# Layer-norm tails that stay in the pixel layout, with bias rows as matmul operands

## Chip, cores and metric

One core of one Trainium2 chip. The metric is the device time of one execution, in microseconds. Engines: PE (matmuls and transposes, with PEld for its weight loads), DVE (vector), ACT (activations), POOL and SP (which issues most DMAs).

## What is computed

Two layers on an input x of 2 x 256 x 128 x 128, both with a residual. The change touches the first layer:

```python
def _branch(x, w_off, w_def, lw, lb, pad, dil):
    off = _conv(x, w_off, pad, dil)
    y = _deform_dw(x, off, w_def, pad, dil)
    return jax.nn.gelu(_ln2d(y, lw, lb), approximate=False)
x1 = _branch(x, off_w1, def_w1, bw1, bb1, 1, 1)
x2 = _branch(x, off_w2, def_w2, bw2, bb2, 9, 9)
x3 = _branch(x, off_w3, def_w3, bw3, bb3, 12, 12)
c = jnp.einsum('bchw,oc->bohw', x, conv_w[:, :, 0, 0]) + conv_b[None, :, None, None]
out = _ln2d(x1 + x2 + x3 + c, n1_w, n1_b)
h = out.transpose(0, 2, 3, 1)
h = jax.nn.gelu(h @ mlp_w1.T + mlp_b1, approximate=False) @ mlp_w2.T + mlp_b2
out = _ln2d(h.transpose(0, 3, 1, 2) + out, n2_w, n2_b)
```

`_ln2d` normalises each pixel over its 256 channels. `_deform_dw` samples nine taps per pixel at learned offsets. The inputs hold bw1 to bw3, n1_w and n2_w at one and bb1 to bb3, n1_b and n2_b at zero. The second layer is a 3x3 convolution with ternary weights.

## The kernel before

The program has three stages. **Phase A** (L286 to 445, image after image) normalises x, writes a padded table of pixels to HBM, computes the offsets and stores "hats", the bilinear weights. A short serial part (`missing`) finds pixels whose offsets lie outside the fast path's reach and computes a flag that chooses between a fast and a general path. **Sampling** (`sample_near`, L997 on) does the deformable branches and, woven into them, the *tails*: all that comes behind the sampling in the first layer. **Phase C** (L1415 on) is the second layer.

Sampling runs over units: image, pair of rows `Rt`, branch. A unit has a half for each 128 channels. Per half, PE multiplies tiles of the table with A, a sparse matrix of weights (L1189), ACT takes the results out of PSUM into `ev` (L1201, three buffers), and DVE adds them, weighted, into a ring of rows (L1150; first contributions are ACT's, L1132). A has two buffers, one per unit in turn; behind the matmuls of a unit's second half, `prepare(u + 2)` queues on DVE the products that fill the A of the unit after next (L1088).

A tail handles a group of four rows, 512 pixels, of one image and branch. It starts with channels on partitions. `normalised` (L805) transposes it to pixels on partitions (L824, 8 transposes of 128x128; for the branches four bf16 matmuls add corrections, L832), copies it from PSUM (L840, two copies), takes each pixel's mean and variance on DVE (`bn_stats` L848, `bn_aggr` L850), forms the scale and bias on POOL (L852 to 855, the root as a power of -1/2), scales on ACT (L859, four of 128x256) and transposes back to channels (L871, 8 transposes into two banks). The Gelu follows out of PSUM (L887). The first branch is stored in HBM (`g12d`, L894), the second adds what was stored (`other`, L898, L901) and stores it, the third goes on in `finish`: the 1x1 convolution (pc, L802, added at L927), the addition of `other` (L931), a second norm, the MLP (hp, Gelu L950; h, added at L965), a third norm, and the residual x (L980, L986), with `bn_stats` (L990) for the second layer. So a group has five norms.

The order is written out by hand. Each tail is a generator; `Tail.advance` is one step and is called four times a unit, at the start and in the middle of each half's matmuls. `yield n` lets the chain rest for n steps; a second number states how many big tiles it will hold after. A chain starts five steps (LAG) behind the unit that completes its rows. Two units of each branch complete a group, so a group's share is 6 units, 24 steps. `NORMS` bounds the norms under way, `VBUFS` (9) the big tiles, `PEAK` the share of them that is kept for the oldest chain. `pin` keeps an instruction at its place in program order; POOL's operations and the DMAs are not pinned. Banks for the tails come from a ring of four (`bank`).

## Time and profile before

| | |
|---|---|
| median of 3 runs | 7081.11 us (7073.98 to 7081.29) |
| the profiled execution, own time | 7081.61 us |
| its span, first to last instruction | 7079.8 us |
| mean granted PE clock | 0.98 |
| busy: PE, PEld, DVE, ACT, POOL | 94%, 71%, 83%, 66%, 11% of the span |
| phase A | to about 980 us |
| sampling with tails | about 990 to 6033 us |
| phase C | 6033 us to the end |
| matmuls L1189 | 17424 instructions, 3230.6 us busy |
| additions into the rings L1150 | 6372 instructions, 2481.9 us busy |

A fp32 matmul stands in the trace as two instructions, a transpose as one. The profile gives for each engine when it is busy, for each group of instructions the mean time of one, and for each idle time what ended it ("<- ACT ev L1201": it waited until ACT had written ev). Busy time is a union, so overlapping instructions count once; a group's mean can be longer than its share of the union.

### The profile page before, as it was taken

To read this page: it belongs to the slowest core of one execution; us is meant where nothing else is said; L and a number is where in the kernel's file an instruction comes from. 1 tells how busy PE (TensorE), PEld (TensorE's weight loads), DVE (VectorE), ACT (ScalarE), POOL (GpSimd) and SP (SyncE) were. 2 spreads that over 40 slices of the span, in tenths; PEclk is the share of its full clock that TensorE was granted. 3 is DMA by queue.
4 is the path that set the end of the run, shared out by engine and by line. 5 is a ranking of instruction groups with operands and counts; after the bars stand their busy time and mean duration, and the time that the engine had idled before them with its cause. 6 is when DMAs were issued, how large, how long until landed. Compare 5 with 4: busy or idle time off the path is not lost. (4 is left out here: it accounts for less than half of the span.)

```text
span 7079.8 us, 104564 instructions
## 1 busy us (share of the span) xinstructions
PE 6688.0 (94%) x33906; PEld 5042.6 (71%) x33906; DVE 5865.6 (83%) x13020; ACT 4663.3 (66%) x9398; POOL 799.2 (11%) x1307
## 2 busy tenths in 40 slices
PE   6899968999999999999999999999999999899999
PEld 3455558888888888888778888888888885344444
DVE  7766658999989999998679999989999985876775
ACT  2344437788888878887777788888878876332332
POOL 0000010111111111112111111111111111000000
PEclk9999979999999999999999999999999999999999
DMA  8876657777777777776567777777777762221211
GB/s 283 260 207 184 189 149 219 222 217 211 214 213 215 218 211 221 211 210 198 178 187 221 212 219 211 213 214 216 216 210 218 215 201 89 100 81 69 75 70 51
DMA packets 671956, 1330.30 MB, mean 188 GB/s; under 512 B 109736, under 2 KB 290008, under 8 KB 667168
## 3 DMA queue, kind: packets, MB, share of 16 engines
q1 hardware_dynamic: 653408, 1288.49, 61.4%
q10 hardware_dynamic: 17408, 33.56, 1.5%
q8 instruction: 273, 4.47, 0.3%
q14 instruction: 291, 2.38, 0.1%
q0 software_dynamic: 576, 1.39, 0.1%
HBM read 1057.07 MB, written 266.08 MB: 187 GB/s over the span
## 5 line engine op out<-in xcount | busy, mean ns | idle before, releaser
L1189 PE MATMUL pm<-A,xs 96*128 96x216 f32 (+2 forms) x17424 | 3230.6, 339 | 162.6 <-ACT ev L1201 100.9
L1189 PEld LDWEIGHTS pm<-A,xs 96*128 96x128 f32 x17424 | 3017.8, 192 | 417.6 <-issue 174.0
L1150 DVE SCALAR_TENSOR_TENSOR ring<-ev,defw,ring 128x256 f32<-128x256 f32 (+4 forms) x6372 | 2481.9, 450 | 170.6 <-ACT ev L1201 114.6
L1201 ACT COPY ev<-pm 128x432 f32<-128x432 f32 (+4 forms) x4488 | 2000.2, 482 | 552.8 <-PE pm L1189 427.1
L1088 DVE TENSOR_TENSOR A<-hy,hx 96x768 f32<-96x768 f32 (+1 forms) x1124 | 1005.7, 943 | 279.1 <-PE pm L1189 223.0
L1486 PE MATMUL pc<-cring,signs 128*128 128x512 bf16 x4608 | 1005.5, 381 | 20.0 <-ACT cring L1433 13.3
L1486 PEld LDWEIGHTS <-signs 128*128 128x128 bf16 x4608 | 452.0, 98 | 572.9 <-issue 27.5
L859 ACT ACTIVATE T<-T,rs 128x256 f32<-128x256 f32 x1280 | 663.1, 592 | 25.6 <-POOL rs L855 25.6
L852 POOL TENSOR_SCALAR rs<-mv 128x4 f32<-128x4 f32 x320 | 125.2, 391 | 4213.7 <-DVE mv L850 3038.7
L802 PE MATMUL hp<-T,w 128*128 128x512 f32 x1024 | 482.3, 594 | 2.3 <-ACT T L937 2.3
L329 PE MATMUL pz<-wz,xa 128*128 128x486 f32 x1024 | 468.4, 586 | 14.5 <-DVE zr L336 14.3
L848 DVE BATCH_NORM_STATS2 st<-T 128x6 f32<-128x256 f32 x1280 | 446.9, 410 | 30.6 <-ACT T L840 30.5
L802 PE MATMUL h<-hT,w 128*128 128x512 f32 x1024 | 460.7, 593 | 0.0
L1132 ACT ACTIVATE ring<-ev,defw 128x256 f32<-128x256 f32 (+1 forms) x856 | 404.7, 485 | 24.2
L1494 ACT ACTIVATE o<-xl,l1b 128x1024 f32<-128x1024 f32 x64 | 73.5, 1148 | 503.0 <-DMA out_x<-o 451.0
L854 POOL TENSOR_TENSOR rs<-rs,mhalf 128x4 f32<-128x4 f32 x320 | 395.7, 1237 | 0.0
L840 ACT COPY T<-tp 128x512 f32<-128x512 f32 x640 | 343.7, 593 | 64.1 <-PE tp L832 49.1
L1433 ACT CAST cring<-D 128x2048 bf16<-128x2048 f32 (+1 forms) x140 | 245.0, 1755 | 181.8 <-PE pc L1486 121.9
L871 PE MATMUL zc<-ident,T 128*128 128x128 f32 x2560 | 344.6, 278 | 13.8 <-ACT T L859 9.8
L950 ACT ACTIVATE hT<-hp,b 128x512 f32<-128x512 f32 x256 | 175.9, 687 | 249.7 <-PE hp L802 248.1
L435 ACT ACTIVATE hb<-ph 96x512 f32<-96x512 f32 (+1 forms) x384 | 214.1, 593 | 183.6 <-PE ph L428 170.6
L871 PEld LDWEIGHTS zc<-ident,T 128*128 128x128 f32 x2560 | 304.0, 143 | 30.9 <-ACT T L859 13.3
(208 smaller groups left out, 5715.7 us busy)
## 6 DMA issues: line engine op xcount, KB each, us to landing
hy<-hats SPq DMA_DIRECT2D x1112, 288.0 KB
hx<-hats SPq DMA_DIRECT2D x1112, 288.0 KB
xs<-tables SPq DMA_DIRECT2D x1452, 96.0 KB
g12d<-T SPq DMA_DIRECT2D x128, 512.0 KB
other<-g12d SPq DMA_DIRECT2D x128, 512.0 KB
hats<-hb SPq DMA_DIRECT2D x64, 720.0 KB
hats<-hb SPq DMA_DIRECT2D x64, 576.0 KB
xl<-x1d SPq DMA_DIRECT2D x56, 640.0 KB
```

The costliest lines, as they stand in the source:

```text
L329: nc.tensor.matmul(pz[:, 0:NZ], lhsT=xt[:, c, r, :], rhs=k["wz"][:, c, :], start=c == 0, stop=c == KC - 1,)
L802: nc.tensor.matmul(out, lhsT=w, rhs=v, start=i == 0, stop=i == n - 1)
L848: pin(nc.vector.bn_stats(st[:, j, :], Tv[:, j, :]))
L854: nc.gpsimd.tensor_tensor(rs[:, 0, :], rs[:, 0, :], mhalf[:, 0:NB4], ALU.pow)
L859: nc.scalar.activation(Tv[:, j, :], Tv[:, j, :], AF.Identity, scale=rs[:, 0, j : j + 1], bias=rs[:, 1, j : j + 1],)
L871: nc.tensor.transpose(zc[:, j * P : (j + 1) * P], Tv[:, j, c * P : (c + 1) * P], ident)
L1088: nc.vector.tensor_tensor(dst, hy[:, i0:i1].rearrange("p i t w -> p t i w"), hx[:, i0:i1].rearrange("p i t w -> p t i w"), ALU.mult,)
L1132: pin(nc.scalar.mul(dst, src, w))
L1150: pin(nc.vector.scalar_tensor_tensor(dst, src, w, dst, ALU.mult, ALU.add))
L1189: nc.tensor.matmul(pv[:, j, :, m0:m1, :], lhsT=xts[b, Rt][t][:, c * P : (c + 1) * P], rhs=A[:, y0:y1, m0:m1, AO + t * CI : AO + (t + 1) * CI],
L1201: nc.scalar.copy(dst.rearrange("p m (t j) -> p t m j", j=CI), pm[:, 0 : len(ts), 0:n].rearrange("p t (m j) -> p t m j", j=CI),)
L1486: nc.tensor.matmul(pc[:, bank, :], lhsT=w[:, m * P : (m + 1) * P], rhs=xc[:, i, k, t * JC : (t + 1) * JC, kx : kx + W], start=j == 0, stop ...
```

## The change

The branch tails and the norms keep pixels on partitions from the first transpose on. The Gelu is applied in the activation that scales. The partial sums in `g12d` are stored in that layout, contiguous per partition. The products pc1 and h2 take the pixels as the stationary operand and the weights as the moving one, in pieces of 256 columns, so that they come out with pixels on partitions; their biases enter as one more product, of a matrix of ones with a matrix that holds the bias as three bf16 parts in its first rows, padded to 128 rows. The sums are added to the tile a step behind the products. The affine parts of the branch norms and of n1 are left out of the fast path; a comparison of bw, bb, n1w and n1b with one and zero goes into the flag that chooses the general path (which keeps the old class `Tail`). Two of POOL's four operations per norm move to DVE, and the scaling comes seven steps behind the moments instead of five. `NORMS` and `PEAK` go from 3 to 4.

```diff
-NORMS = 3
+NORMS = 4
-PEAK = 3
+PEAK = 4
+    ones3 = const.tile([P, P], BF16, name="ones3")
+    nc.vector.memset(ones3, 1.0)
+    row3 = const.tile([P, 2, C], BF16, name="row3")
+    convb3, b23 = row3[:, 0, :], row3[:, 1, :]
+    def split_rows(pool):
...
+        nc.sync.dma_start(rows, t["rows"].partition_broadcast(P))
+        nc.vector.memset(sel, 0.0)
+        for i in range(3):
+            nc.vector.tensor_copy(part, rows)
+            nc.vector.scalar_tensor_tensor(
+                sel, part, ident[:, i : i + 1], sel, ALU.mult, ALU.add
+            )
+            nc.vector.tensor_tensor(rows, rows, part, ALU.subtract)
+        nc.vector.tensor_copy(row3, sel)
...
+        odd = small.tile([P, 8 * KC], F32, name="odd", tag="odd")
...
+        nc.vector.tensor_reduce(anyodd, odd, AX.X, ALU.max)
+        nc.vector.tensor_tensor(miss["worst"], miss["worst"], anyodd, ALU.max)
...
+    class PixelTail(Tail):
+        def moments(self, rows):
...
+            for j in range(n):
+                pin(nc.vector.bn_stats(st[:, j, :], rows[j]))
+            for j in range(n):
+                pin(nc.vector.bn_aggr(mv[:, j, :], st[:, j, :]))
+            rs = pool.tile([P, 2, n], F32, name="rs", tag="rs", bufs=NORMS)
+            pin(nc.vector.tensor_scalar(rs[:, 0, :], mv[:, :, 1], LN_EPS, None, ALU.add))
+            pin(nc.vector.tensor_scalar(rs[:, 1, :], mv[:, :, 0], -1.0, None, ALU.mult))
+            nc.gpsimd.tensor_tensor(rs[:, 0, :], rs[:, 0, :], mhalf[:, 0:n], ALU.pow)
+            nc.gpsimd.tensor_tensor(rs[:, 1, :], rs[:, 1, :], rs[:, 0, :], ALU.mult)
+            return rs
+        def scaled(self, rows, rs, func):
+            for j, row in enumerate(rows):
+                self.pin(
+                    nc.scalar.activation(
+                        row, row, func, scale=rs[:, 0, j : j + 1], bias=rs[:, 1, j : j + 1]
+                    )
+                )
...
+        def product(self, name, S, bias, pairs, h):
+            bank = self.bank(name).rearrange("p (j c) -> p j c", c=C)
+            for j in range(2):
+                px = slice((2 * h + j) * P, (2 * h + j + 1) * P)
+                self.pin(
+                    nc.tensor.matmul(bank[:, j, :], lhsT=ones3, rhs=bias, start=True, stop=False)
+                )
+                for i, (v, w) in enumerate(pairs):
...
+                            bank[:, j, :], lhsT=v[:, px], rhs=w,
...
+            Sh = S[:, 2 * h : 2 * h + 2, :]
+            def add():
+                self.pin(nc.vector.tensor_tensor(Sh, bank, Sh, ALU.add))
+            return add
...
+        def branch(self, b, br, g, y):
...
+            self.turned(vv, y, (b, br, g))
+            self.read.add((b, br, g))
+            rs = self.moments(rows)
+            yield 7, min(1 + br, 2)
+            self.scaled(rows, rs, AF.Gelu)
+            self.norms -= 1
+            if br == 0:
+                yield 2
+                nc.sync.dma_start(gv, vf)
+                return
+            other = self.tile("other")
+            of = other.rearrange("p k n -> p (k n)")
+            nc.sync.dma_start(of, gv)
+            if br == 1:
+                yield 2
+                pin(nc.vector.tensor_tensor(vf, vf, of, ALU.add))
+                yield 2
+                nc.sync.dma_start(gv, vf)
+                return
+            yield 1, 3
+            xn = self.tile("xn")
+            nc.sync.dma_start(xn, xv)
+            yield 2
+            pin(nc.vector.tensor_tensor(vf, vf, of, ALU.add))
+            yield 2, 2
...
+            yield 1
+            pairs = [(xn[:, c, :], convs[b][:, c, :]) for c in range(KC)]
+            adds = [self.product("pc1", vv, convb3, pairs, h) for h in range(2)]
+            yield 1, 1
+            for add in adds:
+                add()
+            yield 2
+            yield from self.entered()
+            rs = self.moments(rows)
+            yield 7
+            self.scaled(rows, rs, AF.Identity)
+            self.norms -= 1
+            yield 2, 2
+            S = self.tile("S")
+            for c in range(KC):
+                pin(nc.scalar.copy(S[:, c, :], self.channels(rows, c)))
+            yield 1, 3
...
+                yield 1, 4 if m < MC - 1 else 3
+            pairs = [(hT[m // KC][:, m % KC, :], w2[:, m, :]) for m in range(MC)]
+            add = self.product("h2", vv, b23, pairs, 0)
+            yield 1, 3
+            add()
+            add = self.product("h2", vv, b23, pairs, 1)
+            yield 1, 1
+            add()
+            yield 2, 2
+            yield from self.entered()
+            rs = self.moments(rows)
+            xr = self.tile("xr")
+            nc.sync.dma_start(xr, xv)
+            yield 7
+            self.scaled(rows, rs, AF.Identity)
+            self.norms -= 1
...
+            yield 2
+            for c in range(KC):
+                zc = self.channels(rows, c)
...
-        tail = Tail(pool, psum, pin)
+        tail = PixelTail(pool, psum, pin)
```

`turned` is the first part of the old `normalised`, up to the copies out of PSUM, as a method of its own; `channels` does the 4 transposes of one half of the channels that were L871.

More of the change, by code (lines that the diff above doesn't have):

```diff
@@ L91, in conv_preact_kernel, with tmp @@
     nc.vector.memset(mhalf, -0.5)
+    ones3 = const.tile([P, P], BF16, name="ones3")
[3 more added lines that the diff above has]
+    def split_rows(pool):
+        def tmp(name, dt=F32):
+            return pool.tile([P, 2, C], dt, name=name, tag="xt", bufs=3)
+        rows, part, sel = tmp("rows"), tmp("part", BF16), tmp("sel")
+        nc.sync.dma_start(rows, t["rows"].partition_broadcast(P))
[7 more added lines that the diff above has]
+        nc.vector.tensor_copy(row3, sel)
     later = []
@@ L502, in conv_preact_kernel @@
                 nc.vector.tensor_copy(k["hatw"], hatw)
+                split_rows(ap)
                 pattern = ap.tile([P, NG], F32, name="pattern", tag="xt", bufs=3)
@@ L741, in conv_preact_kernel @@
         ids = miss["ids"]
+        odd = small.tile([P, 8 * KC], F32, name="odd", tag="odd")
+        for i, (v, usual) in enumerate(((bw, 1.0), (bb, 0.0))):
+            nc.vector.tensor_scalar(
+                odd[:, 3 * KC * i : 3 * KC * (i + 1)], v.rearrange("p b k -> p (b k)"), usual,
+                None, ALU.not_equal,
+            )
+        for i, (v, usual) in enumerate(((n1w, 1.0), (n1b, 0.0))):
+            nc.vector.tensor_scalar(
+                odd[:, (6 + i) * KC : (7 + i) * KC], v, usual, None, ALU.not_equal
+            )
+        anyodd = small.tile([P, 1], F32, name="anyodd", tag="anyodd")
+        nc.vector.tensor_reduce(anyodd, odd, AX.X, ALU.max)
+        nc.vector.tensor_tensor(miss["worst"], miss["worst"], anyodd, ALU.max)
         farall = small.tile([P, 1], F32, name="farall", tag="farall")
@@ L803, in matmul, with turned @@
                 )
-        def normalised(self, z, src, what=None):
-            pool, pin = self.pool, self.pin
+        def turned(self, Tv, src, what):
+            pin = self.pin
             NB4 = NG // P
-            while self.norms == NORMS:
-                yield 1
-            self.norms += 1
-            T = self.tile("T")
-            Tv = T.rearrange("p k n -> p (k n)").rearrange("p (j c) -> p j c", c=C)
             S = self.spots.get(what and what[0::2])
@@ L843, in normalised @@
                 )
+        def normalised(self, z, src, what=None):
+            pool, pin = self.pool, self.pin
+            NB4 = NG // P
+            while self.norms == NORMS:
+                yield 1
+            self.norms += 1
+            T = self.tile("T")
+            Tv = T.rearrange("p k n -> p (k n)").rearrange("p (j c) -> p j c", c=C)
+            self.turned(Tv, src, what)
             self.read.add(what)
@@ L994, in finish, with entered, channels @@
             )
+    class PixelTail(Tail):
+        def moments(self, rows):
+            pool, pin = self.pool, self.pin
+            n = len(rows)
+            st = pool.tile([P, n, 6], F32, name="st", tag="st", bufs=NORMS)
+            mv = pool.tile([P, n, 2], F32, name="mv", tag="mv", bufs=NORMS)
+            for j in range(n):
[14 more added lines that the diff above has]
+                    )
+                )
+        def entered(self):
+            while self.norms == NORMS:
+                yield 1
+            self.norms += 1
+        def product(self, name, S, bias, pairs, h):
[4 more added lines that the diff above has]
+                    nc.tensor.matmul(bank[:, j, :], lhsT=ones3, rhs=bias, start=True, stop=False)
+                )
+                for i, (v, w) in enumerate(pairs):
+                    self.pin(
+                        nc.tensor.matmul(
+                            bank[:, j, :], lhsT=v[:, px], rhs=w,
+                            start=False, stop=i == len(pairs) - 1,
+                        )
+                    )
+            Sh = S[:, 2 * h : 2 * h + 2, :]
+            def add():
+                self.pin(nc.vector.tensor_tensor(Sh, bank, Sh, ALU.add))
+            return add
+        def channels(self, rows, c):
+            zc = self.bank("zc")
+            for j, row in enumerate(rows):
+                self.pin(
+                    nc.tensor.transpose(
+                        zc[:, j * P : (j + 1) * P], row[:, c * P : (c + 1) * P], ident
+                    )
+                )
+            return zc
+        def branch(self, b, br, g, y):
+            pin = self.pin
+            gv = g12d[b].rearrange("c f -> (c f)").rearrange("(g p e) -> g p e", p=P, e=KC * NG)[g]
+            xv = x[b].rearrange("(k p) h w -> p k (h w)", p=P)[:, :, g * NG : (g + 1) * NG]
+            yield from self.entered()
+            v = self.tile("v")
+            vf = v.rearrange("p k n -> p (k n)")
+            vv = vf.rearrange("p (j c) -> p j c", c=C)
+            rows = [vv[:, j, :] for j in range(NG // P)]
+            self.turned(vv, y, (b, br, g))
[24 more added lines that the diff above has]
+            for c in range(KC):
+                pin(
+                    nc.scalar.activation(
+                        xn[:, c, :], xn[:, c, :], AF.Identity, bias=negmean[b][:, c : c + 1]
+                    )
+                )
+            yield 1
+            pairs = [(xn[:, c, :], convs[b][:, c, :]) for c in range(KC)]
[14 more added lines that the diff above has]
+            yield 1, 3
+            hT = []
+            for m in range(MC):
+                if m % KC == 0:
+                    hT.append(self.tile("hT"))
+                hp = self.bank("hp")
+                self.matmul(hp, [(w1[:, c, m * P : (m + 1) * P], S[:, c, :]) for c in range(KC)])
+                pin(
+                    nc.scalar.activation(
+                        hT[-1][:, m % KC, :], hp, AF.Gelu, bias=b1[:, m : m + 1]
+                    )
+                )
+                yield 1, 4 if m < MC - 1 else 3
[7 more added lines that the diff above has]
+            yield 2, 2
+            yield from self.entered()
+            rs = self.moments(rows)
[4 more added lines that the diff above has]
+            self.norms -= 1
+            for c in range(KC):
+                pin(
+                    nc.scalar.activation(
+                        xr[:, c, :], xr[:, c, :], AF.Identity, bias=n2b[:, c : c + 1]
+                    )
+                )
+            yield 2
+            for c in range(KC):
+                zc = self.channels(rows, c)
+                pin(
+                    nc.vector.scalar_tensor_tensor(
+                        xr[:, c, :], zc, n2w[:, c : c + 1], xr[:, c, :], ALU.mult, ALU.add
+                    )
+                )
+                pin(nc.vector.bn_stats(stats2[b][:, c, g, :], xr[:, c, :]))
+            yield 2, 1
+            nc.sync.dma_start(
+                x1d[b].rearrange("(k p) f -> p k f", p=P)[:, :, g * NG : (g + 1) * NG], xr
+            )
@@ L1614 @@
         "misc": misc,
+        "rows": np.stack([l0["conv_b"], l0["mlp_b2"]]),
         "tapid": np.tile(np.arange(1, NTAP + 1, dtype=np.float32), (P, 1)),
```

## Prediction

> **What bounds the kernel now.** I read the time slices first (part 2 of the page): from slice 7 to slice 33 PE and DVE both stand at 8 or 9 tenths, so the shares of the whole span decide nothing. I then asked for the busy time in three stretches in the middle of the sampling stage. The columns are length, busy us and count of PE, weight loads, DVE, ACT, POOL, then the granted PE clock, the DMA share and GB/s:

> ```profile
> 1500.00:2000.00 500.00, 491.24 (x2584) 418.11 (x2583) 462.98 (x1122) 410.95 (x864) 82.06 (x132) 1.00 0.74 215
> 2000.00:2500.00 500.00, 491.06 (x2549) 413.04 (x2548) 460.99 (x1120) 401.91 (x840) 81.72 (x128) 1.00 0.73 214
> 2500.00:3000.00 500.00, 491.35 (x2588) 418.27 (x2587) 460.16 (x1115) 411.08 (x862) 82.70 (x132) 1.00 0.73 215
> ```

> PE is busy 98.2% at full clock, DVE 92.3%, ACT 82%. Third, who waits in 1500 to 3000 us, PE and DVE:

> ```profile
> PE pm L1189 <- ACT ev L1201: 23.4, 39, 0.8
> ...
> DVE A L1088 <- PE pm L1189: 74.9, 20, 3.7
> DVE ring L1150 <- ACT ev L1201: 27.8, 19, 1.9
> ```

> PE waits 24 us in 1500; DVE waits 75 us for PE, once per group of rows (20 times), always before it builds A. So PE bounds the stage, and DVE has 7.7% in hand. Fourth, the timeline of one period between two such waits (start, duration, engine, line):

> ```profile
> 1885.48 2.69 DVE L1088 TENSOR_TENSOR A<-hy,hx 96x768 f32<-96x768 f32 x3 [3.74 <-PE pm L1189]
> ...
> 1924.01 2.69 DVE L1088 TENSOR_TENSOR A<-hy,hx 96x768 f32<-96x768 f32 x3
> ...
> 1930.32 0.60 PE L832 MATMUL tp<-extra,S 128*128 128x256 bf16 x4
> 1930.75 1.99 PE L1189 MATMUL pm<-A,xs 96*128 96x216 f32 x10
> 1932.58 1.88 PE L802 MATMUL hp<-T,w 128*128 128x512 f32 x4
> 1934.30 2.36 PE L1189 MATMUL pm<-A,xs 96*128 96x216 f32 x12
> ...
> 1948.68 3.60 PE L802 MATMUL h<-hT,w 128*128 128x512 f32 x8
> ...
> 1962.28 1.04 PE L824 MATMUL tp<-ident,ring 128*128 128x128 f32 x8
> 1962.48 2.69 DVE L1088 TENSOR_TENSOR A<-hy,hx 96x768 f32<-96x768 f32 x3 [3.75 <-PE pm L1189]
> ```

> The period is 1962.48 - 1885.48 = 77.0 us: six sampling units, one group's tail. Call the units U0 to U5, U0 behind the wait. The MLP's products (7 us of hp, 7 us of h) crowd into U4 and U5; there PE falls behind and DVE waits 3.74 us. In U0 to U3 it is DVE that is late: it builds without a wait from 1885.48 to the end of U2's build, 1924.01 + 2.69 = 1926.70. I call these 41.2 us the DVE run. There are two A tiles, so U4's first pm needs U2's build. Today it starts at 1930.75, 4 us later, hence PE is the later one. From there to 1962.28 are the 31.5 us of the PE run.

> **What the change takes from PE.** Per group three branches lose the transposes back, two norms the transposes forward: 5 x 8 = 40, at 1.04 us for 8 (above) 5.2 us. The products pc1 and h2 become twice as many of half the width. The stream is the same if 256 columns take half of 512: h pitch is (1952.12 - 1948.68)/8 = 0.43 us, and the pm matmuls of 216 columns run at 2.36/12 = 0.197, which scales to 0.21 to 0.23. I take no change. Added are 8 bf16 bias products: 0.107 (four of L832 in 0.43 before the next starts) to 0.19 (a weight load's mean) each, 0.9 to 1.5, I take 1.2. Net -4.0 us of 75.6 busy.

> **ACT.** Per group six Gelu out of PSUM (0.78) and four copies (0.59) go, some 7 us; the Gelu moves into the 128x256 activations that exist (0.59 as Identity). ACT is not the bound, so this counts nothing, but PE's few waits for ev (1.2 us per group) can't grow from it.

> **DVE.** Ten small operations per group come over from POOL. Nearest rows: bn_aggr, four in 0.36 us, 0.09 each; the 128x2 operations of the group norm 0.17; far off, the same operation on POOL, 0.39. I take 0.12, close to the DVE rows. The additions of pc1 and h2 stay two each, plain tensor_tensor instead of L927's 744 ns, nearest the 681 ns of L1466. The two additions of `other` stay at 1.2 us. One set of moments is 1.6 us now (1891.13 to 1892.73 in the timeline) and becomes 1.85.

> **DMA and waits.** Loads and stores of g12d keep number and size and become 4 KB runs per partition; xn, xr, x1d keep theirs. The load of `other` is issued right behind the Gelu, two steps ahead of its addition in the second branch, as now, where that addition waits under 1 us in 1500. SP is queued on the DVE builds today; nothing here lengthens that queue by an instruction. The new wait is of the Gelu and scalings for POOL's pow, seven steps behind: 7 x 77.0/24 = 22 us, against about 2.5 us on POOL plus the few us by which DVE is late. ACT has the next pm evacuation behind it, but the slack covers that. The 2 banks held by a product for a step are reused four banks later, at the earliest one step behind.

> **The place decides, not the sum.** Count the yields in steps (four per unit) from the turn of the third branch, at U4's first step. Today hp comes in U4's second to fourth step and U5's first, h2 in U5's second and third. After: S's transposes in U4's second, hp in U4's third and fourth and U5's first and second, h2 in U5's third and fourth. All six stay in the PE run. It loses one set of back transposes (-1.04), takes in the set of S that now lies just ahead of it (+1.04) and 4 biases (+0.6): 32.1 us. PE from U0 to U4's first pm was 1930.75 - 1885.28 = 45.5; it loses five sets (5.2) and gains 4 biases (0.6): 40.9. The DVE run today holds tail work of 3.2 (two moments) + 2.55 (L927, L931) + 5.5 (moments, 2.76 for zc's, L901) = 11.25. After: U0 gets the second half's addition 0.7, two moments 3.7, the addition of the third branch 1.15; U1 1.4; U2 one set of moments 1.85, L901 1.15, 2.76: 12.7. So the run grows by 1.45 to 42.65. With 0.2 us for each hand-over (1962.28 to 1962.48) the period is max(40.9, 42.85) + 32.1 + 0.2 = 75.2 us, 1.8 less, not the 4.0 that PE is spared: PE then waits about 2 us for A at U4.

> **Sum**, against the profiled execution's own 7081.61 us (span 7079.8), 0.5 us above the median of 7081.11. Steady stretches 1300-3300 and 3800-5850 us are 4050/77.0 = 52.6 periods: -95. At the change of image, 3300-3600, DVE is 67 to 75% busy and PE 93 to 97%, so the full 4.0 counts for about four groups: -16. The drain (5850-6033, PE 156 of 183 us) has some four groups of tail work: -15. Groups before 1300: -5. In phase A the bias rows add about ten DVE operations of 128x512 (0.5 to 0.7 us each, some 6 us); DVE is 68% and PE 87% busy from 177 to 1240, so most hides: +4 (0 to 8); the oddity flags +1, six operations of 0.15 us. Total -126: **6955 us**.

> **Rivals.** (B) *PE's sum rules*: if the DVE run stays under 40.9, the period is 73.2: -3.8 x 52.6 - 31 = 6850. Against it: 41.2 is measured today, before anything is added. (C) *Nothing is left*: at POOL's 0.39 us the six small operations in the DVE run cost 1.6 more, and a bias of 0.3 us adds 0.6: period 42.85 + 1.6 + 32.7 + 0.2 = 77.4, 7081.6 + 0.4 x 52.6 - 31 = 7072. That the edit is only cosmetic is no rival: the instructions go. (D) *Slower, by the clock*: PE now idles 1.4 us per period and no wait is over 0.8; the new pause of 2 us at U4 comes right ahead of the PE run. In this trace the clock is 1.00 in steady stretches, but 0.91 in 3400-3500 us with PE 96% busy, and 0.90 in 5900-5950. At 0.93 the run takes 34.5, the period 77.6, and everything gained is gone; at 0.88 it takes 36.5, period 79.5, +2.5 x 52.6 - 31 = +100: 7180; at 0.91, 35.3, +1.3 x 52.6 - 31 = +37: 7119. For it: the row at 3400; against it: PE stays 97% busy.
> [...]

> **Chances.** A, the forecast, with a period of 74.5 to 76.7 and so 6915 to 7045 us: 0.60. B (6845 to 6915): 0.16. C, within 0.2%, about what a measurement here can tell from no change: 0.09. D: 0.15. Faster is A and B, 0.76. The range of 8 in 10 leaves out half of B and most of D above 7105: 6880 to 7105.

> **What would show it.** Right: PE's first pm of U4 waits about 2 us per period for DVE's A; DVE's wait for PE before A is still there once per group, shorter by the 1.8 gained less the work added, near 2.5 us; periods of about 75 us; DVE near 96%, PE near 95% busy. Wrong: no PE wait for A and a period of 73 (B); small DVE operations of 0.3 us or more (C); a clock under 0.95 between 1500 and 3000 (D). The weakest term is the DVE run: 1 us there is 53 us of the result.

## The result, and the profile after

The changed kernel takes 7133.39 us (median of 5 runs, 7117.26 to 7141.64) against 7081.11 us for the kernel before in the same series: ratio 1.0074, 95% interval 1.0056 to 1.0092. It is slower by 0.74%; the forecast was 6955 us.

The profiled execution of after took 7141.21 us (span 7139.4 us, mean PE clock 0.964), 59.6 us more than that of before. Three landmarks split this: the flag between phase A and sampling is reduced at 967.28 us (961.66 before, +5.6), the statistics that close sampling come at 6095.69 us (6039.16, so the stage between grew from 5077.5 to 5128.4, +50.9), and the rest, phase C, is 3.1 us longer. The question is sampling. The busy time of after in the three stretches that the prediction showed of before (length, PE, weight loads, DVE, ACT, POOL, clock, DMA share, GB/s):

```profile
1500.00:2000.00 500.00, 473.13 (x2481) 424.09 (x2480) 451.63 (x1148) 362.40 (x772) 60.11 (x64) 0.98 0.73 210
2000.00:2500.00 500.00, 469.40 (x2452) 421.65 (x2451) 456.83 (x1151) 364.21 (x777) 58.10 (x62) 0.97 0.74 210
2500.00:3000.00 500.00, 473.86 (x2471) 422.44 (x2470) 456.99 (x1168) 361.12 (x766) 58.64 (x64) 0.98 0.74 210
```

PE's share fell from 98.2% to 94.4% in the mean of the three, DVE's from 92.3% to 91.0%, and the clock from 1.00 to 0.98: nobody is the bound by its busy time any more, so it is a wait. The waits of PE and DVE from 1500 to 3000 us (total, times, longest):

```profile
PE pm L1405 <- ACT ev L1417: 55.7, 57, 2.1
PE tp L852 <- DVE ring L1366: 23.3, 18, 3.0
...
DVE A L1304 <- PE pm L1405: 113.0, 19, 6.8
```

Against before, the waits for ev have more than doubled (23.4 us, longest 0.8) and a new wait has come, of the transposes of a turned tail for ring rows, once a period. DVE's wait ahead of A grew from 74.9 to 113.0 us: PE, with less to do, comes later to the place where DVE waits for it. Both engines wait for each other once a period. The timeline of one period shows how (start, duration, engine, line):

```profile
1901.60 2.69 DVE L1304 TENSOR_TENSOR A<-hy,hx 96x768 f32<-96x768 f32 x3 [5.59 <-PE pm L1405]
...
1941.37 2.67 DVE L1304 TENSOR_TENSOR A<-hy,hx 96x768 f32<-96x768 f32 x3
1943.97 6.66 DVE L1366 SCALAR_TENSOR_TENSOR ring<-ev,defw,ring 128x256 f32<-128x256 f32 x16
...
1945.11 0.71 PE L852 MATMUL tp<-ident,ring 128*128 128x128 f32 x5
1946.77 0.55 PE L852 MATMUL tp<-ident,ring 128*128 128x128 f32 x3 [0.95 <-DVE ring L1366]
1947.16 0.60 PE L860 MATMUL tp<-extra,S 128*128 128x256 bf16 x4
1947.59 1.63 PE L1405 MATMUL pm<-A,xs 96*128 96x216 f32 x8
...
1979.61 1.04 PE L852 MATMUL tp<-ident,ring 128*128 128x128 f32 x8
1979.81 2.69 DVE L1304 TENSOR_TENSOR A<-hy,hx 96x768 f32<-96x768 f32 x3 [6.37 <-PE pm L1405]
```

The DVE run is 1901.60 to 1941.37 + 2.67 = 1944.04: 42.44 us (forecast 42.65). The PE run is 1947.59 to 1979.61: 32.0 us (forecast 32.1). Between them lie 3.55 us that the forecast set at 0.2. U2's build is done at 1944.04, but U4's first pm stands in PE's order behind the turn of the third branch (L852), and that needs rows of the ring which DVE adds *behind* U2's build: PE does five transposes, stops for the rest, and starts U4 at 1947.59. 42.44 + 3.55 + 32.0 + 0.2 = 78.2 us, the period that is read off (1979.81 - 1901.60).

The same turn stands at the same place in the kernel before, in lines that the prediction passed over:

```profile
1926.62 6.67 DVE L1150 SCALAR_TENSOR_TENSOR ring<-ev,defw,ring 128x256 f32<-128x256 f32 x16
...
1928.57 1.04 PE L871 MATMUL zc<-ident,T 128*128 128x128 f32 x8
1929.44 1.04 PE L824 MATMUL tp<-ident,ring 128*128 128x128 f32 x8
```

In after, the sixth transpose starts 2.8 us into the 16 additions (1946.77 - 1943.97). In before, 2.8 us into them is 1929.42, and the sixth transpose stands at about 1930.0: some 0.6 us of room, where the prediction saw 4.

A second thing is new. Once a period ACT does, in one step, four scalings and the two bias activations of xr, and PE runs out of free banks (the timeline, and behind it the clock, the column before the last two, in stretches of 2.5 us):

```profile
1927.13 2.09 ACT L1064 ACTIVATE v<-v,rs 128x256 f32<-128x256 f32 x4
1929.11 1.33 ACT L1194 ACTIVATE xr<-xr,n2b 128x512 f32<-128x512 f32 x2
...
1930.89 2.98 PE L1405 MATMUL pm<-A,xs 96*128 96x216 f32 x8 [1.93 <-ACT ev L1417]
```

```profile
1926.60:1929.10 2.50, 2.36 (x15) 2.15 (x13) 2.50 (x4) 2.50 (x6) 0.00 (x0) 1.00 0.01 3
1929.10:1931.60 2.50, 0.70 (x3) 0.68 (x4) 2.50 (x7) 2.50 (x6) 0.00 (x0) 0.92 1.00 263
1931.60:1934.10 2.50, 2.50 (x10) 2.25 (x9) 2.50 (x11) 1.46 (x5) 0.00 (x0) 0.50 0.98 254
1934.10:1936.60 2.50, 2.50 (x16) 2.50 (x16) 2.39 (x8) 0.84 (x2) 1.93 (x2) 0.90 0.78 225
```

A wait of 1.93 us, and right behind it PE runs at half clock. The loss is (0.08 + 0.50 + 0.10) x 2.5 = 1.7 us of full clock. In this period it falls into the DVE run and costs nothing, as PE waits for DVE at the hand-over anyway. The mean of 20 periods from 1508 to 3082 us is 78.66, not 78.2, but that is mostly not the clock. The DVE run is 42.45 us in every other period and 42.97 or 43.48 in the rest, which have four or eight DVE instructions more; its mean is 42.79. From the end of U2's build to the end of the period it is 35.76 us in 18 of the 20, with a fall of the clock ahead in each of them; only two periods, of 36.23 and 37.44 us there, pay for one.

### The profile page after: what moved, and what is told of

It is laid out like the page before. It is cut to its first block, busy times and chain, and to the rows that moved or that the text cites. A ratio compares the mean times of both kernels' runs of the same rounds, so it can differ in the third digit from the quotient of the medians.

```text
span 7139.4 us, 102825 instructions
## 1 busy us (share of the span) xinstructions
PE 6584.0 (92%) x33394; PEld 5179.8 (73%) x33394; DVE 5918.9 (83%) x13678; ACT 4295.3 (60%) x8758; POOL 603.2 (8%) x667
## 5 line engine op out<-in xcount | busy, mean ns | idle before, releaser
L1405 PEld LDWEIGHTS pm<-A,xs 96*128 96x128 f32 x17424 | 3087.4, 196 | 416.3 <-ACT ev L1417 241.8
L1366 DVE SCALAR_TENSOR_TENSOR ring<-ev,defw,ring 128x256 f32<-128x256 f32 (+4 forms) x6372 | 2481.9, 452 | 87.9 <-ACT ev L1417 42.4
L1056 POOL TENSOR_TENSOR rs<-rs,mhalf 128x4 f32<-128x4 f32 x320 | 453.8, 1418 | 4485.9 <-DVE rs L1055 3982.2
L1064 ACT ACTIVATE v<-v,rs 128x256 f32<-128x256 f32 x1280 | 664.2, 594 | 13.2 <-POOL rs L1057 13.2
L837 PE MATMUL hp<-S,w 128*128 128x512 f32 x1024 | 482.3, 595 | 0.7 <-ACT S L1163 0.7
L1084 PE MATMUL h<-w,hT 128*128 128x256 f32 x2048 | 477.8, 379 | 0.4 <-ACT hT L1172 0.4
L1050 DVE BATCH_NORM_STATS2 st<-v 128x6 f32<-128x256 f32 x1280 | 446.8, 411 | 20.7 <-ACT v L868 20.7
L1084 PEld LDWEIGHTS h<-w,hT 128*128 128x128 f32 x2048 | 369.3, 190 | 62.9 <-issue 1.3
L1650 DVE TENSOR_TENSOR D<-D,cring 128x2048 f32<-128x2048 f32 (+1 forms) x70 | 146.8, 2105 | 205.1 <-ACT cring L1649 205.1
L350 PEld LDWEIGHTS pz<-wz,xa 128*128 128x128 f32 x1024 | 190.4, 196 | 167.6 <-issue 136.0
L1084 PE MATMUL pc<-convw,xn 128*128 128x256 f32 x1024 | 273.7, 396 | 18.2 <-ACT xn L1144 15.1
```

Source lines behind the costliest of these rows:

```text
L350: nc.tensor.matmul(pz[:, 0:NZ], lhsT=xt[:, c, r, :], rhs=k["wz"][:, c, :], start=c == 0, stop=c == KC - 1,)
L837: nc.tensor.matmul(out, lhsT=w, rhs=v, start=i == 0, stop=i == n - 1)
L1050: pin(nc.vector.bn_stats(st[:, j, :], rows[j]))
L1056: nc.gpsimd.tensor_tensor(rs[:, 0, :], rs[:, 0, :], mhalf[:, 0:n], ALU.pow)
L1064: nc.scalar.activation(row, row, func, scale=rs[:, 0, j : j + 1], bias=rs[:, 1, j : j + 1])
L1084: nc.tensor.matmul(bank[:, j, :], lhsT=v[:, px], rhs=w, start=False, stop=i == len(pairs) - 1,)
```

## The experiments

Theory **R** went into all of the first four runs: the period is DVE run + hand-over through the turn's ring rows + PE run. e1 sets it against **C**: the wait behind ACT's long step brings the clock down, and that costs. e2 and e3 set it against **P**: the busy sums decide, so that work which is only moved changes nothing. Means of periods are of 20 between 1490 and 3130 us. Line numbers shift by a few between kernels. Each ratio is to the kernel before, with its 95% interval.

**e1, the third branch's turn two steps later** (its root is then used five steps behind, in the old step):

```diff
+            if br == 2:
+                yield 2
             yield from self.entered()
...
-            yield 7, min(1 + br, 2)
+            yield 7 if br < 2 else 5, min(1 + br, 2)
```

> The third branch's chain turns its tile two steps later (U4's third step) and scales five steps behind its moments instead of seven, so that everything behind it stays where it is. Theory R (ring): in the changed kernel PE stands at the start of U4 in the turn of the third branch, which needs the ring rows that DVE adds behind U2's build; the period is the DVE run 42.4 + 3.6 (additions, transposes) + the PE run 32.0 + hand-overs = 78.2. With the turn behind 22 of U4's matmuls PE goes on at U2's build: 42.4 + 0.2 + (32.0 + 1.3 for the turn, now inside the run) + 0.2 = 76.1, 2.6 less per period, some -135 us: 7000. Theory C (clock): what was lost comes from the lower granted clock behind PE's pauses, and the turn's place doesn't matter: within 20 us of 7133.

Measured: 7086.36 us, ratio 1.0003 (0.9993 to 1.0013). PE's waits from 1500 to 3000 us:

```profile
PE pm L1407 <- ACT ev L1419: 63.3, 73, 2.1
...
PE pm L1407 <- DVE A L1306: 3.4, 4, 0.9
```

The wait for ring rows is gone. In 6 of 20 periods the clock is 1.00 all through, and they take 76.2 to 77.2 us, which is 33.75 behind U2's build where it was 35.76: R holds. The other 14 hold a fall of the clock and take 77.7 to 78.1 us. Of R's 135 us only 47 came: now that PE no longer waits for DVE at the hand-over, the slow stretch costs.

**e2, two small operations of each norm back on POOL:**

```diff
-            pin(nc.vector.tensor_scalar(rs[:, 0, :], mv[:, :, 1], LN_EPS, None, ALU.add))
-            pin(nc.vector.tensor_scalar(rs[:, 1, :], mv[:, :, 0], -1.0, None, ALU.mult))
+            nc.gpsimd.tensor_scalar(rs[:, 0, :], mv[:, :, 1], LN_EPS, None, ALU.add)
+            nc.gpsimd.tensor_scalar(rs[:, 1, :], mv[:, :, 0], -1.0, None, ALU.mult)
```

> The two small operations per norm go back from DVE to POOL. Theory R: three of the five norms lie in the DVE run; a set of moments takes 1.93 us with them and 1.60 without, so the run is 1.0 shorter and the time 50 us shorter: 7080. Theory P (the small operations don't matter, DVE has 7% idle): within 15 us of 7133.

Measured: 7112.21 us, ratio 1.0044 (1.0029 to 1.0058), between the two. Periods of 77.1 us alternate with longer ones of up to 79.8. The short ones are what R gives; most of the long ones hold a stretch of low clock that reaches behind the hand-over (the mean clock of the profiled execution is 0.965).

**e3, the second branch's addition seven steps later:**

```diff
             if br == 1:
-                yield 2
+                yield 9
                 pin(nc.vector.tensor_tensor(vf, vf, of, ALU.add))
```

> The second branch adds what was stored seven steps later, so 1.15 us of DVE's work leaves U2 (inside the DVE run) for U4 (where DVE waits for PE anyway). Nothing else moves. Theory R: 1.15 us per period, 52 periods: 7073. Theory P (busy sums decide): no work is saved, so within 15 us of 7133.

Measured: 7130.44 us, ratio 1.0073 (1.0052 to 1.0093). Again periods of 77.1 us, which is 78.2 less the addition's 1.15, alternate with longer ones of up to 79.8. The time is P's number, within 3 us of after, but not for P's reason. The DVE run is 1.14 us shorter in the mean (41.65 against 42.79), as R has it; but in 10 of 20 periods a stretch of low clock reaches behind the hand-over and adds 1.2 to 1.7 us there.

**e4, roots used five steps behind in every norm:**

```diff
-            yield 7, min(1 + br, 2)
+            yield 5, min(1 + br, 2)
...
-            yield 7
+            yield 5
```

(the last twice, for the second and third norm)

> The scalings come five steps behind the moments again in all norms, so the MLP comes a unit earlier against the turn of the third branch: its products lie in U3 and U4, and no turn stands ahead of U3's first matmul. Theory R: the DVE run then goes from U4's build to U1's and holds 14.4 us of tail work instead of 12.7, 44.3 us; the PE run is 32: period 76.7, 2.0 less, some -100 us: 7030. Rival: the seven steps were needed, ACT waits for POOL: 7133 or more.

Measured: 7410.72 us, ratio 1.0473 (1.0453 to 1.0493). The waits from 1500 to 3000 us:

```profile
ACT v L1064 <- POOL rs L1057: 65.1, 18, 3.7
...
PE pm L1405 <- ACT v L1064: 59.5, 18, 3.7
```

The rival is right: with five steps ACT waits for POOL's root up to 3.7 us, PE waits behind ACT, and the period is 82 us. The clock is part of it: each of PE's 20 waits of 2.6 us and more is followed by a fall, and its mean over the profiled execution is 0.947 (0.964 in after). Five steps are too few with this order; six were not tried.

**e5, only ACT's long step split:** xr's bias one step behind the scalings, the transposes where they were.

```diff
             self.scaled(rows, rs, AF.Identity)
             self.norms -= 1
+            yield 1
             for c in range(KC):
...
-            yield 2
+            yield 1
```

> The changed kernel with one edit: in the third norm the two bias activations of xr come one step behind the four scalings instead of in their step (the transposes stay where they were). Nothing in the work or in the order of DVE changes. Theory C (ACT's 2.1 + 1.3 us in one piece keep PE from its banks for 1.95 us once in a period, and the granted clock is about 0.5 for the 4 us that follow): PE's waits for ev fall from 55.7 us in 57 to under 20 in 1500 to 3000 us, the clock is 1.00 there, no period is over 78.3, and 0.5 us in each of 52.6 periods go: 7105 us (7090 to 7115). Rival (the pause and the clock fall into time in which PE would wait anyway, the ring's hand-over is all): the pause goes, the time stays within 10 us of 7133.

Measured: 7224.77 us, ratio 1.0204 (1.0187 to 1.0221). Neither theory gave this: the repair costs 91 us. (The 0.5 us a period that theory C wanted back came mainly from the DVE run, as said above.) The timeline and the clock at the hand-over of one period of it:

```profile
1952.11 0.71 PE L852 MATMUL tp<-ident,ring 128*128 128x128 f32 x5
1956.68 0.90 PE L852 MATMUL tp<-ident,ring 128*128 128x128 f32 x3 [3.87 <-DVE ring L1367]
```

```profile
1954.00:1956.50 2.50, 0.00 (x0) 0.00 (x0) 2.50 (x7) 0.38 (x1) 0.00 (x0) 0.91 0.82 262
1956.50:1959.00 2.50, 2.32 (x10) 2.00 (x11) 2.48 (x7) 0.95 (x2) 0.00 (x0) 0.50 1.04 285
1959.00:1961.50 2.50, 2.50 (x9) 2.31 (x8) 2.41 (x5) 0.98 (x3) 0.00 (x0) 0.50 0.66 178
1961.50:1964.00 2.50, 2.50 (x15) 2.37 (x14) 2.50 (x5) 1.59 (x3) 0.00 (x0) 0.72 0.52 135
```

The wait behind ACT is gone, but PE's work didn't grow, and DVE's run is as long as it was. So PE comes to the turn earlier and waits there, 3.87 us in one piece (0.95 in after, in this period). Behind it the clock is 0.5, and here that is the PE run, which nothing hides: the period is 81.1 us in the mean. This gives theory **C'**: as long as PE has less work than DVE's run leaves it time, it must wait somewhere; a single wait of about 2 us or more (1.93 in after, 3.87 here) can halve the clock behind it, and the place of the wait decides whether the slow stretch is hidden (in the DVE run) or paid (in the PE run).

**e6, e1 and e5 together:**

> Both repairs: the third branch's turn two steps later (as in the first run) and xr's bias one step behind the scalings. With the first alone the time was 7086, with periods of 76.2 where the clock was 1.00 and of 77.2 to 78.1 where it was not. Theory R + C: all periods are 76.2, 1.6 us under the first run's mean, in 52.6 periods 84 us less: 7002 us (6985 to 7025). Rival (the clock falls for another reason, the pause is a bystander): the periods stay between 76.2 and 78.1, 7086 within 12.

Measured: 7084.37 us, ratio 1.0002 (0.9993 to 1.0012): e1's time, so the rival's number, with 17 of 20 periods at 77.9 to 78.9 us. But the cause fits C', as the hand-over in one period shows:

```profile
2005.12 3.05 PE L1408 MATMUL pm<-A,xs 96*128 96x216 f32 x10 [2.14 <-ACT ring L1351]
```

The wait behind ACT went, and one of 2.14 us came at U4's first pm (the prediction's place; the name given is that of ACT's ring row, which ends at 2005.10; A's build ends at 2004.97, 0.15 us ahead of PE's start; in 11 of the 19 periods the name given is A's). Behind it the clock is 0.81 and 0.51 in two stretches of 2.5 us (from 2004.50). Behind U2's build such a period takes 35.42 us, and the three periods without a fall take 33.75.

**e8, e6 and the late addition of e3:** DVE's run gets 1.15 us shorter, and so does PE's wait.

> The two repairs and the addition of the second branch seven steps later, with the small operations left on DVE. Theory R: 76.2 - 1.15 = 75.05 in a period, 7002 - 60 = 6942 us (6925 to 6965). Rival (the addition's new place, in the part where PE sets the pace, holds up the ring there): no less than 7002.

Measured: 6985.26 us, ratio 0.9868 (0.9851 to 0.9885). PE's longest waits from 1500 to 3000 us:

```profile
PE pm L1408 <- ACT ev L1420: 33.8, 59, 0.9
PE pm L1408 <- DVE A L1307: 18.4, 20, 1.4
```

No wait over 1.4 us is left, the clock is 1.00 in all three stretches, and the periods are 75.3 to 75.6 us, taken two at a time. 1.15 us out of DVE's run took 99 us off the time; by R alone it is 60 (1.15 x 52.6). The clock that stays up is worth more: in the mean of 20 periods the part behind U2's build went from 35.17 us to 33.75, 75 us in 52.6 periods. The two together are more than was measured; where the other 36 us went was not followed. Expected were 6942. The 75.05 put down is the short period (75.07 here); the others have a longer DVE run, and the mean is 75.45.

**e7, all of it** (e8 and the two small operations on POOL, as in e2):

> The two repairs, and the second branch's addition seven steps later and the two small operations of each norm back on POOL, which take 1.15 and 1.0 us out of DVE's run ahead of the hand-over. Theory R (DVE's run, hand-over and PE's run add up, and each us out of DVE's run is a us of the period): 76.2 - 2.15 = 74.05, and 7002 - 113 = 6889 us (6870 to 6920). Rival (PE's own 72.5 to 74.2 us of work in a period is the bound by then, with its waits on top): 75 or more, 6940 us or more.

Measured: 6975.77 us, ratio 0.9853 (0.9836 to 0.9870), the fastest version and faster than both kernels of the case. The first of the three stretches:

```profile
1500.00:2000.00 500.00, 483.92 (x2593) 433.29 (x2592) 472.36 (x1151) 381.99 (x823) 99.89 (x132) 1.00 0.78 220
```

PE is 97% busy at full clock, its wait for A is 0.7 us in 1500 and DVE's for PE 83.7 us. The period is 75.0 us with 72.7 us of PE's work in it. The DVE run still varies by 1.0 us (40.2 to 41.3), but the period only by 0.4 (74.84 to 75.21): the rival was right, PE bounds it, and another us out of DVE's run gives only some 10 us instead of 53, hardly more than the runs differ (6970 to 6981 us, against 6976 to 6990 in e8).

**e9, e8 with ACT's long step put back:** the converse of e5.

> The third branch's turn two steps later and the second branch's addition seven steps later, with xr's bias back in the step of the scalings, as in the changed kernel. Against the same kernel with xr's bias one step behind (6985 us, periods of 75.5, PE's longest wait 1.0 us, clock 1.00) only ACT's 3.4 us in one piece come back. Theory C': one PE wait of 1.95 us returns in each period and the clock falls to about 0.5 for 4 us behind it, together 1.95 - 0.70 + 2.0 us, of which PE's present wait of 1.0 us at the hand-over absorbs 1.0: 2.25 in each period, 7103 us (7040 to 7120). Rival (PE has slack there, a wait in that place is absorbed whole): 6985 within 15.

Measured: 7094.32 us, ratio 1.0020 (1.0010 to 1.0031), 109 us over e8 where C' gave 118. Nothing but the place of two activations of 0.67 us differs. The wait is back (`PE pm <- ACT ev` 66.4 us in 78, longest 2.1), and periods of 76.07 us at clock 1.00 alternate with periods of 77.7 to 78.1 at 0.98. In after the split cost 91 us and here it saves 109: the same edit, with its sign set by what waits behind it. That the number is so near C' is in part luck: C' put a fall of the clock into each period, and 12 of 20 waits had one.

**e10 and e11, the kernel before with a longer step of ACT:** behind the third norm's scalings, 2 or 4 rows are scaled once more.

```diff
             for j in range(NB4):
                 pin(
                     nc.scalar.activation(
                         Tv[:, j, :], Tv[:, j, :], AF.Identity,
                         scale=rs[:, 0, j : j + 1], bias=rs[:, 1, j : j + 1],
                     )
                 )
+            for j in range(extra):
+                pin(
+                    nc.scalar.activation(
+                        Tv[:, j, :], Tv[:, j, :], AF.Identity,
+                        scale=rs[:, 0, j : j + 1], bias=rs[:, 1, j : j + 1],
+                    )
+                )
```

> The kernel before with ACT's piece of work made longer by two: behind the third norm's four scalings the first two rows are scaled once more, in the same step (the values that leave the norm are then others). ACT's piece is 3.1 us, 1.0 more, and PE's wait for ev behind it should be about 1.6 us (3.4 us gave 1.93 in the changed kernel), where none over 0.8 is now. It tells how short a wait still brings the clock down. Theory C' with a limit below 1.6: the clock falls behind it, 1.6 + 2.0 less the 1.3 us that PE is idle now, 2.3 in each of 52.6 periods: 7200 us (7150 to 7240). With a limit above 1.6 the clock stays 1.00 and the time at 7080 to 7115. Rival (ACT's work is free, no wait appears): 7081 within 15.

> The kernel before with all four rows of the third norm scaled once more in the same step: ACT's piece is 4.15 us, 2.1 more, and PE's wait behind it about 2.7 us. Theory C' (a wait of PE of 2 us or more halves the clock for some 4 us behind it, in any kernel): 2.7 + 2.0 less the 1.3 us of idle time that is there now, 3.4 in each of 52.6 periods: 7260 us (7200 to 7300), and the clock 0.5 in one stretch of every period where it is 1.00 now. Rival (the falls of the clock belong to the changed kernel, by its small weights or its mix of work, and not to the wait): the clock stays 1.00 and the time at 7155 (2.7 - 1.3 in each period) or less.

Measured: e10 7147.96 us, ratio 1.0102 (1.0082 to 1.0122); e11 7242.48 us, ratio 1.0232 (1.0208 to 1.0256). In e10 the wait is 0.95 to 1.14 us, shorter than expected, the clock stays 1.00 behind all 19 of them, and the period is 78.1 us, 1.0 more: a short wait costs its own length and no more. The time lies between the numbers put down, which rested on a wait of 1.6 us. In e11 ACT's step and PE's wait are

```profile
1779.95 2.06 ACT L859 ACTIVATE T<-T,rs 128x256 f32<-128x256 f32 x4
1781.92 2.06 ACT L866 ACTIVATE T<-T,rs 128x256 f32<-128x256 f32 x4
...
1784.19 1.72 PE L1196 MATMUL pm<-A,xs 96*128 96x216 f32 x8 [1.93 <-ACT ev L1216]
```

The period is 79.0 us (2.0 more, the whole wait), and behind 5 of 19 waits the clock falls and the period is 80.3 to 80.7. So the fall belongs to the wait and not to the changed kernel's products, but it came less often than in after (18 of 19 there). Of e11's 161 us over before, some 120 are these periods (a mean of 2.3 x 52.6); the rest was not followed. The time alone doesn't decide against the rival, and that it lies in the range of C' is luck: the wait was shorter than the 2.7 us put down and the falls were fewer. The five falls decide.

## Why the prediction was wrong

- **The step that failed** is the hand-over: "There are two A tiles, so U4's first pm needs U2's build. Today it starts at 1930.75, 4 us later, hence PE is the later one." A is one condition of U4's first pm. Another is the order of PE: the turn of the third branch stands ahead of it, and needs ring rows behind U2's build. So the 0.2 us of the hand-over is 3.55 us, the period 78.2 instead of 75.2: 3.0 x 52.6 = 158 us. e1, which takes the turn away from there, has the forecast kind of hand-over, and its short periods at full clock are 76.2 us; the 1.0 above the forecast is the turn's own work, about 1.3 us (1929.44 to 1930.75 in before), which then lies in the PE run.
- **A second step**: "PE's few waits for ev (1.2 us per group) can't grow from it". ACT's sum fell as forecast (411 to 362 us in 500), but its work got lumpier: 3.4 us in one step, and PE's waits for ev grew from 23.4 to 55.7 us. In after this cost little: behind U2's build only two of 20 periods are longer than 35.76 us, 0.1 us in the mean, some 6 us in all. In e1 the same wait took much of the repair's gain.
- **The period read off** is a short one, in the prediction (77.0, where the mean of 20 is 77.13) and here (78.2). The longer DVE run of the others adds 42.79 - 42.44 = 0.35 us in the mean, 18 us. 158 + 6 + 18 = 182, against 178 between forecast and result.
- **DVE run, PE run**: right for the period shown, 42.44 and 32.0 us against 42.65 and 32.1. The moments of a norm cost 1.93 us against the 1.85 put down.
- **PE's saving**: 75.8 to 72.55 us busy a period where the clock is 1.00 (before, e8), 3.2 instead of 4.0. The half-width products take no longer, as forecast: 8 of h in 1.89 us are followed after 1.73 us, 0.216 each, half of 0.43. The 1.04 us that were put down for eight transposes are the length of their row; the next row starts 0.87 us behind it (1928.57 to 1929.44 above), so that forty are 4.4 us and not 5.2. A bias took 0.11 us until the next product began (eight are 0.9, not 1.2). That makes 3.5; the other 0.3 were not split.
- **The other terms**: sampling grew by 50.9 us, of which the periods give (78.66 - 77.13) x 52.6 = 80.5, so the rest gained some 30; forecast were -16, -15 and -5. Phase A grew by 5.6 (forecast +4 and +1). Phase C's 3.1 us were not foreseen.
- **Rival D** named what was to come, a pause of PE of 2 us and a fall of the clock behind it, and its 7119 to 7180 us hold the result. But that is luck: most of the loss, 158 of 182 us, is the hand-over and not the clock, the pause came behind ACT and not at U4, and D's own sign, a clock under 0.95 between 1500 and 3000 us, stayed away (0.98). Rival B's bound by PE's sum is reached only in e7.
- **The signs that were to show it**: no wait of PE for A, which was to be 2 us a period, and no period near 75; DVE's wait ahead of A was to shrink to 2.5 us and is 5.9 in the mean (113.0/19); DVE was to be 96% busy and is 91.0%. These alone say that the forecast's chain is not the one that runs. With the repairs the wait for A does appear (e8: 18.4 us in 20).

## What to carry to other kernels

When an instruction's start is to move, list everything that stands ahead of it in its engine's own order and what each of those needs, and read the room from the nearest of these conditions; one buffer that is ready early says nothing. When an engine that was the bound gets less work, it will wait: ask where, and in how long a piece, since one wait of 1.93 us on PE was followed by a loss of 1.7 us of full clock in after, nearly its length once more, while those of 0.95 to 1.14 us in e10 cost their own length. And spread what another engine has to do in one step if banks come free behind it, but only together with a look at where the wait goes.

## What the runs showed of the hardware

In ten kernels (after, e1, e3 and e5 to e11) every PE wait of 0.85 us or more between 1500 and 3000 us was set against the clock in the 8 us behind it. 65 waits of up to 1.63 us were never followed by a fall of the clock; of 119 waits of 1.8 to 2.2 us, 78 were; all 22 of 2.4 us and more were (18 of them, in e5, are of 3.8 us and more). e2 gives the same picture (none of 4 short waits, 15 of 25 of 1.8 to 2.2 us); in e4 the waits stand too close together to be told apart. These falls have a nearly fixed size: 1.7 us of full clock are lost, as at half clock for 3.4 us, or twice that (in after 18 of 3.41 us and one of 6.83). The 4 us at half clock and the 2.0 us lost that were put down for e5 and e9 to e11 were an estimate; no run shows them. For a wait of about 1.93 us the share goes from 5 of 19 (e11) over 12 of 20 (e9) to 18 of 19 (after).

```profile
1782.14:1785.55 3.41, 1.48 (x9) 1.36 (x9) 2.69 (x8) 3.41 (x9) 0.00 (x0) 1.00 1.04 302
1785.55:1788.97 3.42, 3.42 (x17) 3.35 (x16) 3.37 (x13) 3.39 (x8) 1.57 (x3) 0.50 0.68 172
...
1860.65:1864.06 3.41, 2.11 (x15) 1.73 (x13) 3.41 (x8) 3.41 (x8) 0.00 (x0) 1.00 0.59 178
1864.06:1867.47 3.41, 2.78 (x20) 2.78 (x21) 2.93 (x11) 3.41 (x9) 0.00 (x0) 1.00 1.01 287
1867.47:1870.88 3.41, 3.36 (x19) 3.03 (x18) 3.36 (x13) 3.38 (x9) 2.17 (x4) 1.00 0.45 121
```

The first wait (to 1784.19) lies in one cell, PE is busy for 1.48 of its 3.41 us, and the next cell runs at half clock. The second (to 1864.69) is cut by the edge at 1864.06, PE is busy for 2.11 and 2.78 us, and the clock stays up. In all thirteen kernels together the stretch from 1500 to 3000 us has 5521 cells at full clock. All 124 in which PE was busy for 46.8% or less were followed by half clock, none of the 5379 with 54% or more, and 11 of the 18 between. After alone has 419 such cells: the 19 in which PE was busy for 13.3 to 45.2% were followed by half clock, the 400 with 52.3% and more were not. So in these runs the share that a wait takes of one cell, together with the small gaps around it, goes with the fall; why was not shown.
